# Attention with its scores held transposed, in a four-layer graph network kernel

## The chip, the cores and the metric

The kernel runs on one core of one Trainium2 chip. A core has five engines that work side by side, each through its own queue in order: TensorE (PE in the profile; the loading of its weights is shown apart as PEld), VectorE (DVE), ScalarE (ACT), GpSimd (POOL) and SyncE (SP), which here only starts DMAs. POOL starts DMAs too. SBUF is the on-chip memory with 128 partitions; PSUM is the small memory that TensorE writes its products to[...]. The metric is the device time of one execution in microseconds, lower is better.

## The reference

There are 2708 nodes with 512 features each, and a symmetric 0/1 adjacency matrix with about 0.6% ones. Four layers follow each other; each is `x = layernorm(x + layer(x, adj))`. Layers 0, 1 and 3 multiply the adjacency matrix with x (or with x scaled by the degrees) and then with a 512 x 512 weight matrix. The change is in layer 2, which is two rounds of attention over all pairs of nodes:

```python
def _gat_layer(x, W, adj):              # W: 512 x 1024
    proj = x @ W
    Wh, Ws = jnp.split(proj, 2, axis=-1)
    scores = Wh @ Ws.T                  # 2708 x 2708
    a = jax.nn.softmax(scores, axis=-1) * adj
    out = a @ Wh
    out = out + x
    return jax.nn.leaky_relu(out, 0.01)
x = inputs
for l in range(2):
    x = _gat_layer(x, W_stack[l], adj)
```

The softmax runs over the whole row, before the mask. Its denominator is therefore the sum over all 2708 columns, and not only over the neighbours.

## The kernel before

**Layers 0, 1 and 3** are `aggregated`. It holds x as row blocks of 128 nodes, split into a high and a low part (`xh`, `xl`, both in the fp32r format). The nodes that are summed into are cut into six chunks of at most 512 columns (`CH`: three of 512, two of 384, one of 404). For each chunk the transposed adjacency matrix is loaded by SP in six pieces (`at`, line 476), made into `m` by a copy (line 489), and TensorE adds up four PSUM accumulators `acc` (line 493), with x as the stationary and the adjacency as the moving operand. So the result is transposed, features down the partitions. `project` (line 453) multiplies it with the weights, which turns it back to rows, and the epilogue (`end0`, `end1`, `end3`) does bias, residual and layernorm on DVE. In layers 0 and 1 the rows are written to DRAM (`saved`, line 524), and the next layer loads them again (`xr`, line 383, and `xres`, line 450).

**Layer 2** is `attention`. It loads the 22 row blocks of x, and for each of its two rounds goes through three stages:

- *Projection* (lines 224 to 232). Per row block: four transposes of x (`tr_x`), a copy `xt`, eight matmuls with the halves of W (`mm_ws`, `mm_wh`), the copies `ws` and `z` (the Wh of this block), four transposes of `ws`, and a copy into `wst`, which holds Ws transposed.
- *Scores and softmax* of a row block of 128 queries: `z` is transposed (`wht`, line 143), six column chunks of 452 are multiplied into PSUM (`sp`, line 147), and DVE copies each to the score matrix `s` and takes its row maximum in the same instruction (line 154). Queries lie on the partitions, so the row maximum is one number per partition, `nmax`. ACT takes one exponential over 2708 columns with `nmax` as bias and adds up the row sums on the way (line 172). SP loads the mask and DVE multiplies it in (line 177).
- *Weighing* (`weigh`). The second product needs the keys on the partitions. So the 22 blocks of `s` are transposed on TensorE in groups of four (`etr`, line 191), copied to SBUF by ACT and DVE in turn (`et`), and used as the stationary operand against `z` (`acc`, line 202). `finish` divides by the row sum, adds x and applies the leaky ReLU; in the second round it also adds the layer's input, takes the layernorm and stores the block (lines 210 to 219).

The scores of row block i+1 stand in TensorE's queue before the weighing of block i. All matmuls of this layer are in Float32. A scheduler decides the order in which the instructions stand in each engine's queue, from the dependencies and the order in which they are written. A pool hands out buffers: a tile with `bufs=n` has n buffers in turn, and a new tile waits until the one that used its buffer before is finished with. Between two of the kernel's stages, the pools of the new stage take the memory of the old stage's pools, and wait for all of them.

Of the kernel before, what the change touches and what calls it, by code (L numbers as in the profile page):

```python
# [8 lines left out]
FP = mybir.dt.float32  # L9
# [3 lines left out]
AF = mybir.ActivationFunctionType  # L13
ALU = mybir.AluOpType
AX = mybir.AxisListType
PSUM = bass.MemoryType.PSUM
DRAM = bass.MemoryType.DRAM

P = 128
N = 2708  # L20
D = 512
NB = 22
NP = NB * P
DC = D // P
BANK = 512

CH = [(0, 512), (512, 512), (1024, 512), (1536, 384), (1920, 384), (2304, 404)]
# [7 lines left out]
SLOPE = 0.01  # L35


def rows_of(i):
    return min(P, N - i * P)


class Kernel:


    def __init__(self, ctx, tc, x_in, x_t, adj, adj_t, w0, b0, w1, b1, w2, w3, b3, out):
        self.tc, self.nc = tc, tc.nc
        nc = self.nc
# [17 lines left out]
            [scratch.tile([P, D], FP, tag=f"x{s}_{i}", name=f"x{s}_{i}") for i in range(NB)]  # L65
            for s in range(3)
        ]

# [291 lines left out]
    def aggregated(self, layer, source, weights, bias, epilogue):  # L360
# [4 lines left out]
        with ExitStack() as ctx:  # L365
            pool = lambda name, bufs, **kw: ctx.enter_context(
                tc.tile_pool(name=f"{name}{layer}", bufs=bufs, **kw)
            )
# [3 lines left out]
            ps_mm = pool("ps_mm", 2, space=PSUM)  # L372
            ps_deg = pool("ps_deg", 1, space=PSUM)
            w = self.load_w(hp, weights, D, f"w_{layer}")
            bt = hp.tile([P, D], FP, tag="bias", name=f"bias{layer}")
# [69 lines left out]
            def project(k, ht):  # L445
                c0, cw = CH[k]
                for q in range(-(-cw // P)):
# [4 lines left out]
                    for c in range(DC):  # L452
# [6 lines left out]
                        )  # L459
                    epilogue(i, n, ps, bt, xr)  # L460

            done = None
            for k, (c0, cw) in enumerate(CH):
# [9 lines left out]
                for g, (b0, b1) in enumerate(GROUPS):  # L473
# [26 lines left out]
                    if g == 0 and done is not None:  # L500
                        project(*done)
                ht = hp.tile([P, DC, BANK], FP, tag="ht", name=f"ht{layer}_{k}")
                if layer == 0:
# [6 lines left out]
                done = (k, ht)  # L510
            project(*done)

    def fast(self):
# [20 lines left out]
        def end1(i, n, ps, bt, x):  # L534
            r = self.rows.tile([P, D], FP, tag="r", name=f"r1_{i}")[:n]
            nc.vector.scalar_tensor_tensor(
                r, ps[:n], self.dis[:n, i : i + 1], bt[:n], ALU.mult, ALU.add
            )
            nc.vector.tensor_add(r, r, x[:n])
            normalized(i, n, r, self.saved[1])  # L540

# [8 lines left out]
        self.aggregated(1, self.saved[0], self.w1, self.b1, end1)  # L550
        self.attention(self.saved[1], self.saved[2])
        self.aggregated(3, self.saved[2], self.w3, self.b3, end3)
# [75 lines left out]
```

## Time and profile before

| what | value |
|---|---|
| three runs | 3170.51, 3165.39, 3166.81 us; median 3166.81 |
| profiled run | 3169.31 us, its span 3167.5 us, mean granted TensorE clock 0.984 |
| layers 0 and 1 | 0 to about 660 us of the span |
| attention, first round | TensorE from 671.7 us to 1755 us |
| attention, second round | from 1755 us to 2834 us |
| layer 3 | from 2855 us to the end |
| DMA | 236.93 MB, 75 GB/s over the span |

The profile is one execution. Its page lists the busy time of each engine, the span in 40 slices, the chain of work that ended last (followed back from the last instruction, at each step to what released it), and the costliest groups of instructions. A group's row has its line, engine and operation, output and inputs with their shapes, the count, then the busy time in us, the mean of one in ns, and the idle time of the engine ahead of it. Matmuls overlap in a pipeline and their ends are modelled, so the distance between their starts tells more of their cost than their mean duration.

### The profile page before, as it was taken

How to read it: one execution, taken by the hardware profiler on the slowest of the kernel's cores; microseconds unless marked ns; L12 is line 12 of the kernel's file. 1: busy time of each engine (PE TensorE's matmuls, PEld its weight loads, DVE VectorE, ACT ScalarE, POOL GpSimd, SP SyncE). 2: the span in 40 equal slices, each digit the busy share in tenths (PEclk: the TensorE clock that was granted, in tenths of full speed). 3: DMA queues.
4: the chain of work that ended last, by engine and by line, in shares of the span. 5: the costliest groups of instructions: out<-in, count | busy, mean ns of one | idle time of the engine just before them, and what ended most of it. 6: DMA issues, size and time to landing. Idle time of an engine off the chain costs nothing.

```text
span 3167.5 us, 25252 instructions
## 1 busy us (share of the span) xinstructions
PE 3017.2 (95%) x9974; PEld 1746.5 (55%) x9974; DVE 1057.7 (33%) x2511; ACT 552.9 (17%) x668; POOL 188.9 (6%) x314
## 2 busy tenths in 40 slices
PE   6999799979999999999999999999999999979997
PEld 5677577844454554444444444544444444436785
DVE  7768423221122222222222112333333333333133
ACT  3112332211110011111111111111111111114221
POOL 3112201010000000000000000000000000002000
PEclk9999899989999999999999999999999999999998
DMA  7434654420011111111111000111111111116441
GB/s 256 151 129 143 218 174 131 133 104 0 11 51 35 36 35 35 36 35 36 35 36 35 0 0 18 49 49 49 47 47 45 49 49 49 49 51 239 140 147 58
DMA packets 115138, 236.93 MB, mean 75 GB/s; under 512 B 10406, under 2 KB 69542, under 8 KB 115008
## 3 DMA queue, kind: packets, MB, share of 16 engines
q1 hardware_dynamic: 90432, 152.54, 14.9%
q0 software_dynamic: 24576, 82.68, 7.6%
q8 instruction: 80, 1.31, 0.2%
q14 instruction: 50, 0.41, 0.0%
HBM read 212.32 MB, written 22.85 MB: 74 GB/s over the span
## 4 chain that ended last, share of the span: by engine, by line
PE 89%; DVE 4%; issue 3%; DMA 2%; ACT 1%; POOL 0%; POOLq 0%; SPq 0%; ACTq 0%; DVEq 0%
PE acc L202 26%; PE sp L147 26%; PE acc L493 18%; PE mm L453 6%; PE mm_ws L111 5%; PE mm_wh L111 5%; PE etr L191 2%; DMA xr<-x 1%; DVE r L210 1%; ACT xt L226 1%; DVE wht L143 1%; DMA xr<-in_x 1%; PE tr_x L104 1%; PE tr_ws L104 1%; DVE odd L398 0%
## 5 line engine op out<-in xcount | busy, mean ns | idle before, releaser
L202 PE MATMUL acc<-z,et 128*128 128x512 f32 x1936 | 867.6, 593 | 0.2
L147 PE MATMUL sp<-wst,wht 128*128 128x452 f32 (+1 forms) x2112 | 810.9, 544 | 6.1 <-DVE wht L143 0.8
L493 PE MATMUL acc<-m,xh 128*128 128x512 f32 (+2 forms) x1584 | 592.6, 375 | 69.1 <-DMA xr<-x 21.3
L147 PEld LDWEIGHTS sp<-wst,wht 128*128 128x128 f32 x2112 | 397.8, 190 | 398.8 <-issue 382.4
L493 PE MATMUL acc<-m,xl 128*128 128x512 f32 (+2 forms) x1584 | 584.9, 371 | 6.5 <-DVE xl L386 6.5
L202 PEld LDWEIGHTS acc<-z,et 128*128 128x128 f32 x1936 | 353.8, 190 | 373.7 <-issue 372.6
L493 PEld LDWEIGHTS acc<-m,xh 128*128 128x128 f32 x1584 | 304.2, 192 | 109.0 <-ACT xh L385 43.8
L154 DVE TENSOR_SCALAR_CACHE_REDUCE s<-sp 128x452 f32<-128x452 f32 (+1 forms) x264 | 165.8, 628 | 554.2 <-PE sp L147 554.2
L493 PEld LDWEIGHTS acc<-m,xl 128*128 128x128 f32 x1584 | 303.6, 192 | 46.4 <-DVE xl L386 11.0
L172 ACT ACTIVATE s<-s,nmax 128x2708 f32<-128x2708 f32 x44 | 112.3, 2552 | 723.0 <-DVE nmax L171 723.0
L453 PE MATMUL mm<-w,ht 128*128 128x512 f32 (+1 forms) x528 | 231.6, 596 | 3.2 <-DVE ht L507 3.2
L195 ACT COPY et<-etr 128x512 f32<-128x512 f32 x132 | 77.4, 586 | 750.6 <-PE etr L191 750.6
L193 DVE COPY et<-etr 128x512 f32<-128x512 f32 x132 | 79.2, 600 | 350.7 <-PE etr L191 350.6
L111 PE MATMUL mm_ws<-w,xt 128*128 128x512 f32 x352 | 165.4, 613 | 31.9 <-ACT xt L226 31.9
L191 PEld LDWEIGHTS etr<-ident,s 128*128 128x128 f32 x968 | 118.4, 141 | 94.6 <-issue 94.6
L453 PEld LDWEIGHTS mm<-w,ht 128*128 128x128 f32 (+1 forms) x528 | 98.2, 187 | 125.0 <-issue 112.7
L111 PE MATMUL mm_wh<-w,xt 128*128 128x512 f32 x352 | 158.2, 592 | 0.0
L489 ACT CAST m<-at 128x2048 fp32r<-128x2048 f32 (+2 forms) x72 | 113.4, 1577 | 222.9 <-PE acc L493 206.0
L177 DVE TENSOR_TENSOR s<-s,gat_a 128x452 f32<-128x452 f32 (+1 forms) x264 | 145.3, 619 | 0.0
L191 PE MATMUL etr<-ident,s 128*128 128x128 f32 x968 | 141.6, 273 | 0.0
L111 PEld LDWEIGHTS mm_ws<-w,xt 128*128 128x128 f32 x352 | 64.2, 192 | 107.3 <-issue 64.8
L215 POOL DMA_DIRECT2D xb<-x x22 | 11.9, 539 | 1831.4 <-DVE r L217 1791.3
(90 smaller groups left out, 1392.3 us busy)
## 6 DMA issues: line engine op xcount, KB each, us to landing
gat_a<-in_adj SPq DMA_DIRECT2D x220, 226.0 KB, 3.5
at<-in_adj_t SPq DMA_DIRECT2D x45, 1024.0 KB, 5.1
at<-in_adj_t SPq DMA_DIRECT2D x30, 768.0 KB, 4.4
at<-in_adj_t SPq DMA_DIRECT2D x15, 808.0 KB, 4.5
x<-o POOLq DMA_DIRECT2D x44, 256.0 KB, 2.5
xr<-x POOLq DMA_DIRECT2D x44, 256.0 KB, 5.1
xres<-x POOLq DMA_DIRECT2D x44, 256.0 KB, 2.9
x<-x POOLq DMA_DIRECT2D x44, 256.0 KB, 3.4
```

Of the source, the lines that this page charges most:

```text
L111: self.nc.tensor.matmul(ps, src[:, c, :], w[:, c, lo : lo + D], start=(c == 0), stop=(c == DC - 1))
L147: nc.tensor.matmul(sp[:, :cw], wht[:, c, :], wst[:, c, c0 : c0 + cw], start=(c == 0), stop=(c == DC - 1),)
L154: nc.vector.tensor_scalar(s[:, c0 : c0 + cw], sp[:, :cw], 1.0, None, ALU.mult, ALU.max, accum_out=mx[:, k : k + 1],)
L172: nc.scalar.activation(s[:, :N], s[:, :N], AF.Exp, bias=nmax, accum_out=den)
L177: nc.vector.tensor_mul(s[:, c0 : c0 + cw], s[:, c0 : c0 + cw], a[:, :cw])
L191: nc.tensor.transpose(ps[:, q, :], s[:, bass.ts(c, P)], self.ident)
L193: nc.vector.tensor_copy(et[:, :n, :], ps[:, :n, :])
L195: nc.scalar.copy(et[:, :n, :], ps[:, :n, :])
L202: nc.tensor.matmul(acc, et[:, q, :], z[c], start=(c == 0), stop=(c == NB - 1))
L453: nc.tensor.matmul(ps[:n], ht[:, c, q * P : q * P + n], w[:, c, :], start=(c == 0), stop=(c == DC - 1),)
L489: nc.scalar.copy(m[:, :nb, :cw], at[:, :nb, :cw])
L493: nc.tensor.matmul(acc[d][:, :cw], x[j][:, bass.ts(d, P)], m[:, j - b0, :cw], start=(j == 0 and x is xh), stop=(j == NB - 1 and x is xl),)
```

## The change

Attention is written anew as `scored`, and layer 1 hands x over in another form.

- **Scores transposed.** The work goes by the six chunks `CH` of queries, and within a chunk by 22 blocks j of 128 keys. `sp` has the keys on the partitions and up to 512 queries along the columns. A step's score tile goes to one of 26 buffers of `ring` by an ACT copy; the chunk's 22 tiles are all held, because the maximum over the keys must be known first.
- **Row maxima by transposes.** DVE keeps a running maximum over the tiles (`top`). At the end of a chunk `shift_rows` transposes it on TensorE, reduces it on DVE and spreads it over 128 columns (`wide`); `shift_columns` transposes that back, so that each query's maximum stands on all partitions (`shift`).
- **Softening.** Per tile: DVE subtracts `shift`, ACT takes the exponential, POOL adds it to the running sum `sum`, DVE multiplies by the mask, which SP loads per tile from the transposed adjacency matrix.
- **Second product.** `weigh` uses the masked exponentials as they lie as the moving operand, with slices of `z` as the stationary one, into four accumulators over the key blocks. The transposes `etr` and the copies `et` are gone. `close` sums `sum` over the partitions by a product with ones (`den`), takes the reciprocal, and multiplies, adds x and applies the leaky ReLU on tiles of 128 x 4 x cw, on DVE and POOL.
- **x kept transposed.** In layer 1 the normalized rows stay in SBUF (`lasting`); `turn` transposes them chunk by chunk and stores them to `turned[0]`. The projection loads this form, so that it transposes neither x nor Ws. The first round stores its result to `turned[1]`. In the second round `rows_back` transposes the result to rows for the layernorm and stores them for layer 3.
- **Pools** of `aggregated` and `scored` are opened with `reuse_waits="tile"`: a tile that takes memory of an earlier stage waits only for the tiles that lay there.

The steps are interleaved by hand: at step t the scores of step t, the weighing of step t-25 and the softening of step t-23 are written.

```diff
-                tc.tile_pool(name=f"{name}{layer}", bufs=bufs, **kw)
+                tc.tile_pool(name=f"{name}{layer}", bufs=bufs, reuse_waits="tile", **kw)
...
+            lasting = pool("lasting", 5) if layer == 1 else None
...
+            def turn(k):
+                c0, cw = CH[k]
+                t = ap.tile([P, DC, BANK], FP, tag="xt", name=f"x2t{k}", bufs=1)
+                for q, o in enumerate(finished):
+                    n = min(P, cw - q * P)
+                    ps = ps_deg.tile([P, DC, P], FP, tag="deg", name=f"tr_x2_{k}_{q}")
+                    for c in range(DC):
+                        nc.tensor.transpose(
+                            ps[:, c, :n], o[:n, bass.ts(c, P)], self.ident[:n, :n]
+                        )
+                    nc.scalar.copy(t[:, :, q * P : q * P + n], ps[:, :, :n])
+                nc.gpsimd.dma_start(self.turned[0][k], t[:, :, :cw])
+                finished.clear()
...
+                    if g == 2 and finished:
+                        turn(k - 1)
...
+            keep, ring, work = pool("keep", 1), pool("ring", 26), pool("work", 1)
+            ps_acc = pool("ps_acc", 1, space=PSUM)
+            ps_mm, ps_tr = pool("ps_mm", 2, space=PSUM), pool("ps_tr", 2, space=PSUM)
...
+            def project(layer):
+                w = []
+                for c in range(2 * DC):
+                    t = ring.tile([P, D], FP, tag="s", name=f"w2_{layer}_{c}")
+                    half = bass.ts(c // DC, D)
+                    nc.sync.dma_start(t, self.w2[layer, bass.ts(c % DC, P), half])
+                    w.append(t)
+                for k, (c0, cw) in enumerate(CH):
+                    xt = load_xt(layer, k)
+                    for m in range(DC):
+                        ps = ps_mm.tile([P, BANK], FP, tag="mm", name=f"wst{layer}_{k}_{m}")
+                        for c in range(DC):
+                            nc.tensor.matmul(
+                                ps[:, :cw],
+                                w[DC + c][:, bass.ts(m, P)],
+                                xt[:, c, :cw],
+                                start=(c == 0),
+                                stop=(c == DC - 1),
+                            )
...
+                    for q in range(-(-cw // P)):
+                        i, n = c0 // P + q, min(P, cw - q * P)
+                        ps = ps_mm.tile([P, D], FP, tag="mm", name=f"z{layer}_{i}")
+                        for c in range(DC):
+                            nc.tensor.matmul(
+                                ps[:n],
+                                xt[:, c, q * P : q * P + n],
+                                w[c],
+                                start=(c == 0),
+                                stop=(c == DC - 1),
+                            )
...
+            def turn_wh(layer, k):
+                c0, cw = CH[k]
+                wht = work.tile([P, DC, BANK], FP, tag="wht", name=f"wht{layer}_{k}")
+                for q in range(-(-cw // P)):
+                    i, n = c0 // P + q, min(P, cw - q * P)
+                    ps = ps_tr.tile([P, DC, P], FP, tag="tr", name=f"tr_wh{layer}_{i}")
+                    for c in range(DC):
+                        nc.tensor.transpose(
+                            ps[:, c, :n], z[i][:n, bass.ts(c, P)], self.ident[:n, :n]
+                        )
+                    to = wht[:, :, q * P : q * P + n]
+                    if q % 2:
+                        nc.vector.tensor_copy(to, ps[:, :, :n])
+                    else:
+                        nc.scalar.copy(to, ps[:, :, :n])
+                return wht
...
+            def scores(ch, j):
+                n, cw = rows_of(j), ch.cw
+                ps = ps_mm.tile([P, BANK], FP, tag="mm", name=f"sp{ch.name}_{j}")
+                for c in range(DC):
+                    nc.tensor.matmul(
+                        ps[:n, :cw],
+                        wst[j][:, c, :n],
+                        ch.wht[:, c, :cw],
+                        start=(c == 0),
+                        stop=(c == DC - 1),
+                    )
+                s = ring.tile([P, BANK], FP, tag="s", name=f"s{ch.name}_{j}")
+                ch.s.append(s)
+                nc.scalar.copy(s[:n, :cw], ps[:n, :cw])
+                if j == 1:
+                    ch.top = work.tile([P, BANK], FP, tag="top", name=f"top{ch.name}", bufs=2)
+                    nc.vector.tensor_max(ch.top[:, :cw], ch.s[0][:, :cw], s[:, :cw])
+                elif j > 1:
+                    nc.vector.tensor_max(ch.top[:n, :cw], ch.top[:n, :cw], s[:n, :cw])
+            def shift_rows(ch):
+                nq = -(-ch.cw // P)
+                ps = ps_tr.tile([P, DC, P], FP, tag="tr", name=f"tr_top{ch.name}")
+                for q in range(nq):
+                    n = min(P, ch.cw - q * P)
+                    nc.tensor.transpose(
+                        ps[:n, q, :], ch.top[:, q * P : q * P + n], self.ident
+                    )
+                mx = self.small.tile([P, DC], FP, tag="mx", name=f"mx{ch.name}")
+                wide = work.tile([P, DC, P], FP, tag="wide", name=f"wide{ch.name}")
+                for q0, q1, n in ((0, ch.cw // P, P), (ch.cw // P, nq, ch.cw % P)):
+                    if q0 == q1:
+                        continue
+                    nc.vector.tensor_reduce(mx[:n, q0:q1], ps[:n, q0:q1, :], AX.X, ALU.max)
+                    nc.vector.tensor_copy(
+                        wide[:n, q0:q1, :],
+                        mx[:n, q0:q1].unsqueeze(2).to_broadcast([n, q1 - q0, P]),
+                    )
+                ch.wide = wide
+            def shift_columns(ch):
+                ps = ps_tr.tile([P, BANK], FP, tag="tr", name=f"tr_mx{ch.name}")
+                for q in range(-(-ch.cw // P)):
+                    n = min(P, ch.cw - q * P)
+                    nc.tensor.transpose(
+                        ps[:, q * P : q * P + n], ch.wide[:n, q, :], self.ident[:n, :n]
+                    )
+                ch.shift = work.tile([P, BANK], FP, tag="shift", name=f"shift{ch.name}", bufs=2)
+                nc.scalar.copy(ch.shift[:, : ch.cw], ps[:, : ch.cw])
+            def soften(ch, j):
+                n, cw = rows_of(j), ch.cw
+                s = ch.s[j][:n, :cw]
+                c0 = CH[ch.k][0]
+                a = work.tile([P, BANK], FP, tag="a", name=f"a{ch.name}_{j}", bufs=4)
+                nc.sync.dma_start(a[:n, :cw], self.adj_t[j * P : j * P + n, c0 : c0 + cw])
+                nc.vector.tensor_sub(s, s, ch.shift[:n, :cw])
+                nc.scalar.activation(s, s, AF.Exp)
+                if j == 0:
+                    ch.sum = work.tile([P, BANK], FP, tag="sum", name=f"sum{ch.name}", bufs=2)
+                    nc.gpsimd.tensor_copy(ch.sum[:, :cw], s)
+                else:
+                    nc.gpsimd.tensor_add(ch.sum[:n, :cw], ch.sum[:n, :cw], s)
+                nc.vector.tensor_mul(s, s, a[:n, :cw])
+            def weigh(ch, j):
+                n, cw = rows_of(j), ch.cw
+                if j == 0:
+                    ch.acc = [
+                        ps_acc.tile([P, BANK], FP, tag=f"acc{d}", name=f"acc{ch.name}_{d}")
+                        for d in range(DC)
+                    ]
+                for d in range(DC):
+                    nc.tensor.matmul(
+                        ch.acc[d][:, :cw],
+                        z[j][:n, bass.ts(d, P)],
+                        ch.s[j][:n, :cw],
+                        start=(j == 0),
+                        stop=(j == NB - 1),
+                    )
+            def close(ch):
+                layer, k, cw = ch.layer, ch.k, ch.cw
+                o = work.tile([P, DC, BANK], FP, tag="o", name=f"o{ch.name}")
+                for d in range(DC):
+                    nc.scalar.copy(o[:, d, :cw], ch.acc[d][:, :cw])
+                xt = load_xt(layer, k)
+                ps = ps_tr.tile([P, BANK], FP, tag="tr", name=f"den{ch.name}")
+                nc.tensor.matmul(
+                    ps[:, :cw], self.ones, ch.sum[:, :cw], start=True, stop=True
+                )
+                r = work.tile([P, BANK], FP, tag="r", name=f"r{ch.name}")
+                nc.vector.reciprocal(r[:, :cw], ps[:, :cw])
+                o = o[:, :, :cw]
+                nc.vector.tensor_mul(o, o, r[:, :cw].unsqueeze(1).to_broadcast([P, DC, cw]))
+                nc.gpsimd.tensor_add(o, o, xt[:, :, :cw])
+                nc.vector.scalar_tensor_tensor(o, o, SLOPE, o, ALU.mult, ALU.max)
+                if layer == 0:
+                    nc.gpsimd.dma_start(self.turned[1][k], o)
+                    return
+                first = load_xt(0, k)
+                nc.gpsimd.tensor_add(o, o, first[:, :, :cw])
+                ch.o = o
+            def rows_back(ch):
+                c0, cw = CH[ch.k]
+                for q in range(-(-cw // P)):
+                    i, n = c0 // P + q, min(P, cw - q * P)
+                    ps = ps_tr.tile([P, D], FP, tag="tr", name=f"tr_o{i}")
+                    for c in range(DC):
+                        nc.tensor.transpose(
+                            ps[:n, bass.ts(c, P)], ch.o[:, c, q * P : q * P + n], self.ident
+                        )
+                    t = work.tile([P, D], FP, tag="row", name=f"row{i}", bufs=2)
+                    if n < P:
+                        nc.gpsimd.memset(t, 0.0)
+                    self.layernorm(t[:n], ps[:n])
+                    nc.gpsimd.dma_start(self.saved[2][i], t)
+            LAG = 3
+            for layer in range(2):
+                project(layer)
+                chunks = [Chunk(layer, k) for k in range(len(CH))]
+                chunks[0].wht = turn_wh(layer, 0)
+                steps = [(ch, j) for ch in chunks for j in range(NB)]
+                for t in range(len(steps) + NB + LAG + 1):
+                    if t < len(steps):
+                        ch, j = steps[t]
+                        scores(ch, j)
+                        if j == NB - 1 and ch.k + 1 < len(chunks):
+                            chunks[ch.k + 1].wht = turn_wh(layer, ch.k + 1)
+                    if t >= NB and t % NB == 0 and t // NB <= len(chunks):
+                        shift_rows(chunks[t // NB - 1])
+                    u = t - NB - LAG
+                    if 0 <= u < len(steps):
+                        weigh(*steps[u])
+                    if t >= NB and t % NB == 0 and t // NB <= len(chunks):
+                        shift_columns(chunks[t // NB - 1])
+                    v = t - NB - 1
+                    if 0 <= v < len(steps):
+                        soften(*steps[v])
+                    if 0 <= u < len(steps) and steps[u][1] == NB - 1:
+                        close(steps[u][0])
+                    if layer == 1 and u >= NB and u % NB == 2:
+                        rows_back(chunks[u // NB - 1])
+                if layer == 1:
+                    rows_back(chunks[-1])
...
-            normalized(i, n, r, self.saved[1])
+            o = self.lasting.tile([P, D], FP, tag="x2", name=f"x2_{i}")
+            self.layernorm(o[:n], r)
+            return o
...
-        self.attention(self.saved[1], self.saved[2])
+        self.scored()
```

## The prediction

> **What bounds the kernel now.** I read the page first: busy time, then slices, then the chain, then the groups.
>
> ```profile
> PE 3017.2 (95%) x9974; PEld 1746.5 (55%) x9974; DVE 1057.7 (33%) x2511; ACT 552.9 (17%) x668; POOL 188.9 (6%) x314
> ...
> PEclk9999899989999999999999999999999999999998
> ...
> PE 89%; DVE 4%; issue 3%; DMA 2%; ACT 1%; POOL 0%; POOLq 0%; SPq 0%; ACTq 0%; DVEq 0%
> PE acc L202 26%; PE sp L147 26%; PE acc L493 18%; PE mm L453 6%; PE mm_ws L111 5%; PE mm_wh L111 5%; PE etr L191 2%; DMA xr<-x 1%; DVE r L210 1%; ACT xt L226 1%; DVE wht L143 1%; DMA xr<-in_x 1%; PE tr_x L104 1%; PE tr_ws L104 1%; DVE odd L398 0%
> ...
> L202 PE MATMUL acc<-z,et 128*128 128x512 f32 x1936 | 867.6, 593 | 0.2
> L147 PE MATMUL sp<-wst,wht 128*128 128x452 f32 (+1 forms) x2112 | 810.9, 544 | 6.1 <-DVE wht L143 0.8
> ...
> L191 PE MATMUL etr<-ident,s 128*128 128x128 f32 x968 | 141.6, 273 | 0.0
> ```
>
> TensorE is on 89% of the chain; in both attention layers it is simply full. The others have room, so only TensorE's own work, and new waits on it, count. The means of 593 and 544 ns are overlapped records, so I price by starts, from the chain of one row block:
>
> ```profile
> 968.25 18.44 PE sp L147 x48
> 986.69 3.43 PE acc L202 x8
> 990.12 0.44 PE etr L191 x4
> ...
> 1007.15 0.75 DVE r L210
> 1007.90 0.61 DVE wht L143
> 1008.51 0.04 issue
> 1008.55 3.68 PE sp L147 x9
> ```
>
> The period is 1008.55-968.25 = 40.30 us: 48 score instructions in 18.44 (0.384 each), 44 weighing ones at 3.44/8 = 0.430 (18.92), and 2.94 for 26 transposes, 0.113 each with their small waits. In the projection a row block takes (859.45-684.75)/20 = 8.735 us, by the mm_ws starts of the chain. A Float32 matmul is two instructions.
>
> The stage's end, from the timeline:
>
> ```profile
> 2833.51 0.75 DVE L210 SCALAR_TENSOR_TENSOR r<-acc,rden,x 128x512 f32<-128x512 f32 x1 [4.66 <-PE acc L202]
> ...
> 2841.55 38.27 SPq L476 DMA_DIRECT2D at<-in_adj_t  x7
> ...
> 2843.38 2.13 POOL L383 DMA_DIRECT2D xr<-x  x4
> ...
> 2854.75 0.80 PE L493 MATMUL acc<-m,xh 128*128 128x512 f32 x1 [21.28 <-DMA xr<-x]
> ```
>
> TensorE stands 21.3 us here; the last store gates the next stage's loads.
>
> POOL's price comes from the groups by form:
>
> ```profile
> L429 POOL TENSOR_TENSOR xt<-xt,dg 128x512 f32<-128x512 f32 x12 | 17.3, 1471 | 65.4 <-DVE cnt_sb L440 65.4
> ```
>
> **What the Trainium skill says.** *Perfetto Trace Analysis*, "Tensor Engine Instruction (MATMUL, LD_WEIGHTS)": a matmul's end is an estimate. The trace agrees: a transpose is shown as 273 ns and starts every 110. *FP8 and Floating Point Precision*, "TensorE Precision Notes": true Float32 takes four passes; the trace has two instructions of 430 ns for 512 columns. *SBUF — State Buffer*, "SBUF: two separate sides": a VectorE operation with two SBUF inputs and a GpSimd operation that reads SBUF exclude each other for their whole length. No row of before shows it; it bounds the slow end below. *VectorE: DVE Perf Modes*, "First, the fixed hardware budget": the reciprocal iterates with a repeat count of 8 at 0.96 GHz; an estimate for 512 columns is 4.3 us. The trace has it only on 1 to 4 columns (0.16 us).
>
> **The change, part by part**, on TensorE, both layers together.
>
> *Scores.* Four products per key block over 2708 queries, as many columns and instructions as before: 0.
>
> *Transposes of the exponentials.* 968 go: -968 x 0.113 = -109.4. Their 264 copies on ACT and DVE lay beside TensorE: 0.
>
> *Second product.* 22 x 4 x 2708 columns instead of 22 x 22 x 512, as 2112 instructions instead of 1936. At the score price, 2112 x 0.384 = 811.4 against 44 x 18.92 = 832.5: -21.1. Narrow 384-column chunks are not in the trace for Float32; if the overhead stays 4 ns instead of 8, 8 us less on each product.
>
> *Projection.* Before 44 x 8.735 = 384.3. Now per layer 192 instructions at 0.384 and 176 at 0.430 = 149.5, no transposes; both 299.0: -85.3. Its eviction (0.59 ACT, 0.69 DVE, or four quarter pieces) stays under the 3.4 us of a product and is hidden.
>
> *Added on TensorE.* Row maxima there and back, 88 transposes: +9.9. Column sums, 24 instructions: +9.2. Output turned back, 88: +9.9. x turned in layer 1, 88, of which 72 lie in its dense part: +8.1. Together +37.1. The sum so far: -178.7.
>
> *Softening.* A step (one key block, 512 queries) gives TensorE 16 x 0.430 = 6.9 us, DVE three operations of 0.69 (2.1), ACT a copy of 0.59 and an exponential of some 0.5, POOL an addition of 1.47, SP one 256 KB load (3.5 us to land). Even one after the other DVE and POOL take 3.5. In the built order softening also runs several steps ahead of weighing. I take 0; below it is impossible, since TensorE is full; above, see the slow rival.
>
> *Turning x (layer 1).* One PSUM buffer: each group of transposes waits for ACT's copy (0.59) of the one before, with 4 to 6 matmuls of 0.22 between. About 1 us per chunk: +5 (0 to 12).
>
> *Chunk seams.* wht has one buffer and acc one set: at a chunk's start the scores wait for four copies, at its end the next weighing for one copy of acc. Mostly three to seven products lie between. 1.5 us at each layer's start, 1 at its first seam, 0.5 at the others, rounded up to 8 a layer: +16 (5 to 40).
>
> *Rows back (second layer).* In the built queue TensorE reaches the turned-back output three steps after a chunk's last weighing. By then must have passed: ACT's four copies 2.3, reciprocal 0.7 to 4.3, DVE product 2.3 (a 2048-column operation, L398, took 2.29), POOL's addition 4 x 1.47 = 5.9, DVE 2.3, POOL again 5.9: 19.4 to 23 us, plus what is queued ahead. Three steps are 20.6 us for the first chunk, 18.2 and 15.7 for the next, 15.9 against a chain three quarters as long, and four weigh-only steps of 2.75 for the fifth. The waits are 0-5, 2-7, 4-9, 0-3, 4-8: I take 16. The second pair of blocks waits for a pair's layernorm in two PSUM buffers, 2 to 3 us: 10. Behind TensorE everything else is queued, so it counts: +26 (5 to 50).
>
> *Start of attention.* x comes turned, chunk by chunk. But in SP's queue the weight loads w2 stand behind a mask load whose buffer waits for the last layernorm, and the fourth of them for the last turned store. On before's clock: layernorm 663.7, transposes and copy 664.8, store landing some 4 us later, five loads to about 674.5. TensorE began at 671.7: +3 (-5 to +6).
>
> *Between the layers.* xt and w2 are there early; DVE's and POOL's closing (some 12 us) lies beside 27 us of projection: 0.
>
> *Layer 0 to 1.* Buffers are waited for one by one, but the first at load waits for DVE's last ht, where it started before (336.5); xr now stands behind the last store in POOL's queue, 5 us later, with less traffic beside it: 0 (-5 to +5).
>
> *End of attention.* After the last weighing (404 columns): copies 0.8, reciprocal about 2, DVE 1.8, POOL 4.0, DVE 1.8, POOL 4.0, transposes 0.9, two paired layernorms about 10, then POOL's w, bias and xr issues (1.9) and their landing, 5; xh and xl 1.3: about 35 us against 21.3, +14. The at loads and casts are then already in, which saves about 4 of the uneven start: +10 (0 to +18).
>
> Waits together +60. Net -178.7+60 = -119: 3167.5-119 = 3049 on the profile's span. The profiled run took 3169.3, the others 3165.4 to 3170.5 (median 3166.8), so span and median agree within 1 us.
>
> **Rivals.** *Waits vanish* (the order leaves more slack than I count; reciprocal 0.7): 18 us of waits remain instead of 60, 3007. For it: every wait stands behind work that I estimated. Against: TensorE takes its queue in order. *Long closings:* reciprocal at 4.3 and POOL and DVE excluding each other stretch both layers' seams and the end by 4 us at each of 11 closings: 3094. *Slower than before:* the exclusion makes the softening step the bound. Where both products run (220 steps, TensorE 6.15 us on average), DVE's 1.9 plus POOL's addition must exceed 6.15; the gain is gone when they reach 6.7, so POOL's addition must take 4.8 us instead of 1.3 (1.47 at 452 of 512 columns). At 5.0 the step is 6.9: 3049+220 x 0.75 = 3214. Against: POOL's row, taken in layer 0, is 1.47 with DVE 75% busy. *The turned x saves nothing*, its weights being late: already in my sum, but should the seams cost the whole gain, no change.
>
> **How the numbers follow.** My sum 0.45 (alone 3025 to 3075), waits vanish 0.23, long closings 0.26, no change 0.02, slower 0.04. So faster 0.94, same 0.02, slower 0.04, where 0.2% is about what a measurement can tell from no change. The range 2998 to 3105 takes in both neighbours.
>
> **What would show it.** Right: no etr; acc and sp 2112 instructions each at starts 0.38 apart on average; layers of about 992 and 1025 us against 1084 and 1078; short TensorE waits on tr_o and 35 us ahead of layer 3; DVE and POOL well under 60% busy. Wrong: TensorE waiting in every step for DVE's masked product, or POOL additions over 3 us.

## The result, and the profile after

The changed kernel takes 3194.22 us (median of four runs, 3192.33 to 3195.24) against 3168.38 us before: a ratio of 1.0082, with a 95% interval of 1.0064 to 1.0099. The forecast was 3049, with a range of 2998 to 3105 and a chance of 0.04 for slower. So the range does not hold the time, and the sign is wrong.

The page of the kernel after, first the busy times, the granted clock, and the groups that answer to those shown of before:

```profile
PE 2921.0 (91%) x9150; PEld 1688.7 (53%) x9150; DVE 1345.0 (42%) x2229; ACT 639.7 (20%) x1080; POOL 615.4 (19%) x568
...
PEclk9999899989999999999999999998989898988999
...
L636 PE MATMUL sp<-wht,wst 128*128 128x512 f32 (+4 forms) x2112 | 866.7, 558 | 46.2 <-ACT s L645 46.2
L709 PE MATMUL acc<-s,z 128*128 128x512 f32 (+4 forms) x2112 | 853.9, 549 | 14.9 <-ACT o L721 9.3
...
L698 POOL TENSOR_TENSOR sum<-sum,s 128x512 f32<-128x512 f32 (+4 forms) x252 | 351.3, 1394 | 124.6 <-ACT s L693 110.0
...
L699 DVE TENSOR_TENSOR s<-s,a 128x512 f32<-128x512 f32 (+3 forms) x264 | 304.4, 1188 | 21.1 <-POOL sum L698 16.7
L692 DVE TENSOR_TENSOR s<-s,shift 128x512 f32<-128x512 f32 (+3 forms) x264 | 240.4, 960 | 35.8 <-ACT shift L683 35.8
```

TensorE has less work (2921 us against 3017), `etr` is gone, and the two products have their 2112 instructions each. But TensorE is no longer full: its share fell from 95% to 91%, and the granted clock drops again and again in attention, where it stayed at 9 before once the first round was under way. The two DVE rows are the odd ones, and their means mix widths. Kept apart by width, an operation on two SBUF tiles took in the kernel before:

```profile
L177 DVE TENSOR_TENSOR s<-s,gat_a 128x452 f32<-128x452 f32 x220 | 121.7, 619 | 0.0
L545 DVE TENSOR_TENSOR r<-r,xres 128x512 f32<-128x512 f32 x21 | 14.5, 690 | 0.2
```

In the kernel after, at 512 columns:

```profile
L698 POOL TENSOR_TENSOR sum<-sum,s 128x512 f32<-128x512 f32 x120 | 189.6, 1580 | 68.4 <-ACT s L693 61.4
L699 DVE TENSOR_TENSOR s<-s,a 128x512 f32<-128x512 f32 x126 | 158.8, 1295 | 9.2 <-POOL sum L698 8.1 <-DMA a<-in_adj_t 1.1
L692 DVE TENSOR_TENSOR s<-s,shift 128x512 f32<-128x512 f32 x126 | 124.0, 1034 | 20.4 <-ACT shift L683 20.4
```

The mask product takes 1.30 us and the subtraction 1.03, where 0.69 was to be expected. POOL's additions, at 1.58, are near the 1.47 that they were priced at.

The same by stage: start and end, length, then busy time (and instructions) of PE, PEld, DVE, ACT, POOL, and the clock. First the two rounds of attention and the stretch ahead of layer 3, in the kernel after:

```profile
684.00:1727.20 1043.20, 999.74 (x2625) 487.43 (x2626) 413.67 (x483) 178.74 (x363) 211.87 (x153) 0.98 0.14 45
1727.20:2855.00 1127.80, 1016.35 (x2696) 502.70 (x2695) 467.36 (x648) 197.11 (x394) 250.66 (x179) 0.94 0.15 46
2855.00:2890.30 35.30, 4.73 (x19) 2.99 (x19) 15.17 (x40) 8.71 (x11) 13.29 (x13) 0.53 0.54 183
```

By TensorE's starts, attention began 12 us later than before (684.0 against 671.7). The first round took 1043 us instead of 1084, where 992 were forecast. The second took 1163 with the stretch ahead of layer 3, where before needed 1099.5 and the forecast was 1060; layer 3 was 9.6 us shorter (303.1 against 312.7). The sum, +12.3 - 40.4 + 63.6 - 9.6, is the 26 us between the spans. TensorE stands idle for 1043.2 - 999.7 = 43.5 us in the first round and 111.4 us in the second, at a clock of 0.98 and 0.94.

Whom it waits for, from TensorE's waits (sum in us, times, longest):

```profile
PE tr_o L747 <- POOL o L737: 54.7, 6, 13.9
PE sp L636 <- ACT s L645: 46.2, 12, 7.8
...
PE tr_o L747 <- DVE row L106: 36.5, 5, 14.6
...
PE tr_o L747 <- DVE ln_r L95: 17.4, 1, 17.4
```

The `tr_o` waits are 108.7 us in all; 17.2 of them belong to the last chunk, after which there is nothing else to do. A closing shows where they come from. This is the timeline of all engines around the first one of the second round, with only the lines of the closing and of what stands beside it:

```profile
2147.41 3.35 DVE L728 RECIPROCAL r<-den 128x512 f32<-128x512 f32 x1
...
2153.58 4.89 POOL L731 TENSOR_TENSOR o<-o,xt 128x2048 f32<-128x2048 f32 x1 [4.62 <-DVE o L730]
2154.03 4.99 DVE L699 TENSOR_TENSOR s<-s,a 128x512 f32<-128x512 f32 x1
...
2159.65 1.23 ACT L693 ACTIVATE s<-s 128x512 f32<-128x512 f32 x2 [11.62 <-DVE s L692]
...
2162.51 4.87 POOL L737 TENSOR_TENSOR o<-o,xt 128x2048 f32<-128x2048 f32 x1 [3.19 <-DVE o L732]
2162.94 4.98 DVE L650 TENSOR_TENSOR top<-top,s 128x512 f32<-128x512 f32 x1
...
2167.43 1.97 PE L747 MATMUL tr_o<-ident,o 128*128 128x128 f32 x8 [7.84 <-POOL o L737]
```

Here POOL twice adds 2048 columns, and beside each addition a VectorE operation of 512 columns takes 5 us instead of 0.68: it ends 0.55 us, about its own length, after POOL does. All nine of POOL's 2048-column additions have such a partner (4.85 to 5.00 us), and it starts 0.26 to 0.45 us after POOL. The product `s<-s,a` has no data in common with `o<-o,xt`. Behind it on VectorE stand the subtractions, behind them ACT's exponentials (11.62 us of idle time), and behind these in ACT's queue the copies of the next scores. From `den` (2135.0) to the last addition (2167.4) the closing takes 32 us; the forecast had 19 to 23.

### The profile page after: what moved, and what is told of

The parts are those of the page before. It is cut to its first block, busy times and chain, and to the rows that moved or that the text cites. A ratio compares the mean times of both kernels' runs of the same rounds, so it can differ in the third digit from the quotient of the medians.

```text
span 3193.4 us, 24534 instructions
## 1 busy us (share of the span) xinstructions
PE 2921.0 (91%) x9150; PEld 1688.7 (53%) x9150; DVE 1345.0 (42%) x2229; ACT 639.7 (20%) x1080; POOL 615.4 (19%) x568
## 5 line engine op out<-in xcount | busy, mean ns | idle before, releaser
L636 PE MATMUL sp<-wht,wst 128*128 128x512 f32 (+4 forms) x2112 | 866.7, 558 | 46.2 <-ACT s L645 46.2
L709 PE MATMUL acc<-s,z 128*128 128x512 f32 (+4 forms) x2112 | 853.9, 549 | 14.9 <-ACT o L721 9.3
L636 PEld LDWEIGHTS sp<-wht,wst 128*128 128x128 f32 (+1 forms) x2112 | 402.1, 192 | 474.6 <-issue 302.7
L709 PEld LDWEIGHTS acc<-s,z 128*128 128x128 f32 (+1 forms) x2112 | 401.3, 192 | 408.7 <-issue 238.0
L650 DVE TENSOR_TENSOR top<-top,s 128x512 f32<-128x512 f32 (+2 forms) x240 | 168.2, 701 | 828.0 <-ACT s L645 827.1
L698 POOL TENSOR_TENSOR sum<-sum,s 128x512 f32<-128x512 f32 (+4 forms) x252 | 351.3, 1394 | 124.6 <-ACT s L693 110.0
L520 PEld LDWEIGHTS acc<-m,xh 128*128 128x128 f32 x1584 | 303.0, 191 | 101.1 <-ACT xh L394 46.4
L699 DVE TENSOR_TENSOR s<-s,a 128x512 f32<-128x512 f32 (+3 forms) x264 | 304.4, 1188 | 21.1 <-POOL sum L698 16.7
L692 DVE TENSOR_TENSOR s<-s,shift 128x512 f32<-128x512 f32 (+3 forms) x264 | 240.4, 960 | 35.8 <-ACT shift L683 35.8
L578 PE MATMUL wst<-xt,w 128*128 128x512 f32 (+2 forms) x384 | 151.9, 555 | 12.3 <-DMA w<-in_w 12.3
L596 PE MATMUL z<-w,xt 128*128 128x512 f32 (+1 forms) x352 | 153.2, 592 | 0.0
L747 PE MATMUL tr_o<-ident,o 128*128 128x128 f32 (+1 forms) x88 | 22.2, 426 | 108.7 <-POOL o L737 54.7
```

Of the source, the lines that this page charges most:

```text
L520: nc.tensor.matmul(acc[d][:, :cw], x[j][:, bass.ts(d, P)], m[:, j - b0, :cw], start=(j == 0 and x is xh), stop=(j == NB - 1 and x is xl),)
L578: nc.tensor.matmul(ps[:, :cw], w[DC + c][:, bass.ts(m, P)], xt[:, c, :cw], start=(c == 0), stop=(c == DC - 1),)
L596: nc.tensor.matmul(ps[:n], xt[:, c, q * P : q * P + n], w[c], start=(c == 0), stop=(c == DC - 1),)
L636: nc.tensor.matmul(ps[:n, :cw], wst[j][:, c, :n], ch.wht[:, c, :cw], start=(c == 0), stop=(c == DC - 1),)
L650: nc.vector.tensor_max(ch.top[:n, :cw], ch.top[:n, :cw], s[:n, :cw])
L692: nc.vector.tensor_sub(s, s, ch.shift[:n, :cw])
```

## The experiments

Three theories were put against each other. **A:** only the place of `rows_back` in the order is wrong, three steps being too few. **B:** VectorE and GpSimd exclude each other, and that holds up the chain from softening to closing. **C:** VectorE is simply short of time. All times are medians; the kernel before stood at 3167 to 3168 us beside each.

**Rows back later** (`e1_late`).

```diff
-                    if layer == 1 and u >= NB and u % NB == 2:
+                    if layer == 1 and u >= NB and u % NB == 12:
```

> Only the place of rows_back in the order: ten steps later (u % NB == 12 instead of 2). Theory A (queue place: TensorE reaches tr_o before the closing chain is done): the tr_o waits of the first five chunks go, 108.7 - 17.2 (the last chunk, which stays) = 91.5 us, and with them some 10 us of TensorE at half clock: 3194 - 100 = about 3094. Theory B (VectorE and GpSimd exclude each other, and the softening is behind because of it): the stalls were also time in which VectorE caught up, so half of it comes back as waits of sp for the copies s: about 3145. Both agree on the first half of attention (no change).

Measured: 3143.11 us, ratio to before 0.9917 (0.9900 to 0.9933). The first round is as it was (684.4 to 1728.5). The first five chunks' waits on `tr_o` are gone, but TensorE's waits now read:

```profile
PE sp L636 <- ACT s L645: 81.7, 19, 14.1
```

That is 81.7 us where it was 46.2: of the 91.5 us of `tr_o` waits, 35.5 came back as waits for the score copies. The kernel gained 51 us, B's half (3145) and not A's whole (3094): the place decides where TensorE stands, and the chain behind it is late wherever it stands.

**The sum on VectorE, the closing's additions on VectorE, and both** (`e2_sumdve`, `e3_closedve`, `e4_nopool`).

```diff
-                    nc.gpsimd.tensor_copy(ch.sum[:, :cw], s)
+                    nc.vector.tensor_copy(ch.sum[:, :cw], s)
...
-                    nc.gpsimd.tensor_add(ch.sum[:n, :cw], ch.sum[:n, :cw], s)
+                    nc.vector.tensor_add(ch.sum[:n, :cw], ch.sum[:n, :cw], s)
```

```diff
-                nc.gpsimd.tensor_add(o, o, xt[:, :, :cw])
+                nc.vector.tensor_add(o, o, xt[:, :, :cw])
...
-                nc.gpsimd.tensor_add(o, o, first[:, :, :cw])
+                nc.vector.tensor_add(o, o, first[:, :, :cw])
```

The first pair of edits alone:

> Only the running sum moved from GpSimd to VectorE (264 additions of about 0.69 us more on VectorE, 182 us). Theory B (exclusion): the subtractions and mask products fall from 0.96 and 1.19 us to about 0.65; TensorE's waits of sp for s (46 us) fall below 15, the tr_o waits by some 10 us a chunk, half clock by half: about 3194 - 31 - 50 - 20 = 3093. Theory A (queue place alone): the chain of the closing is as long as before, about 3190. Theory C (VectorE is the engine that is short): slower, about 3194 + 30.

The second pair alone:

> Only the additions of the closing (2048 columns, 4.9 us each on GpSimd, 18 of them) moved to VectorE at about 2.3 us. Theory B: each closing is shorter by 2.6 us per addition and VectorE is no longer held for 5 us by each: tr_o waits -8 us on each of 6 chunks, sp waits from 46 to about 25: about 3120. Theory A: only 2 x 2.6 us on each of 6 chunks: about 3162. Theory C: slower, about 3200.

Both:

> Both: the running sum and the closing's additions on VectorE, GpSimd only starts DMAs in attention. Theory B: no VectorE operation above its length alone; sp waits under 10 us, tr_o waits of the first five chunks under 20 us together, mean clock 0.975: about 3194 - 40 - 75 - 25 = 3055. Theory A: as with the closing's additions alone, about 3162. Theory C: slower than with either alone.

| kernel | us | ratio to before (95%) |
|---|---|---|
| sum on VectorE | 3043.02 | 0.9598 (0.9582 to 0.9614) |
| closing's additions on VectorE | 3128.63 | 0.9873 (0.9856 to 0.9889) |
| both | 2990.48 | 0.9432 (0.9417 to 0.9448) |

More work for VectorE makes the kernel faster by 204 us, so C is out, and A's 3190 and 3162 are too. B has the direction each time; it was close for the closing (3120 expected), and its gain was 50 us too small for the sum and 65 too small for both. The two edits give 151 and 66 us alone and 204 together: two costs that nearly add. VectorE's mask product is back at its length alone:

```profile
L699 DVE TENSOR_TENSOR s<-s,a 128x512 f32<-128x512 f32 x126 | 86.6, 688 | 0.3
```

The stages of the kernel with both, with the same columns as above:

```profile
683.30:1667.30 984.00, 982.82 (x2625) 484.68 (x2626) 363.66 (x620) 182.15 (x363) 10.34 (x16) 0.99 0.16 48
1667.30:2654.90 987.60, 986.00 (x2697) 488.95 (x2695) 413.69 (x791) 208.55 (x401) 21.77 (x36) 0.99 0.17 53
```

TensorE runs the same instructions, and is idle for 1.2 and 1.6 us. Against the kernel after, the first round is 59.2 us shorter, of which 42.3 was idle time and 16.9 slower matmuls; the second, up to its last weighing, is 140.2 us shorter, 109.8 idle and 30.4 slower matmuls.

**Unrelated work on GpSimd** (`e5_shadow`, `e6_shadowcopy`). Moving the sum took away two things: what GpSimd does beside VectorE, and a wait, since the mask product overwrites the tile that GpSimd reads. Here the first is put back without the second, on top of the kernel with both edits; its second form has `tensor_copy(b, a)` instead.

```diff
                 nc.vector.tensor_mul(s, s, a[:n, :cw])
+                b = work.tile([P, BANK], FP, tag="b", name=f"b{ch.name}_{j}")
+                nc.gpsimd.tensor_add(b[:n, :cw], a[:n, :cw], a[:n, :cw])
```

> The kernel with all additions on VectorE, and 264 extra GpSimd additions of the same shape that read only the mask tile and write a tile that nobody reads; the result is not touched. It parts two reasons why the sum on GpSimd cost so much. Theory B1 (GpSimd's and VectorE's additions exclude each other): VectorE's subtractions and products rise from 0.62 us to 0.9 or more although nothing depends on GpSimd, and the time rises from 2990 towards the 3129 of the run with only the closing's additions moved: 3070 to 3130. Theory B2 (the mask product overwrites the tile that GpSimd still reads, so it waits in the queue for it): lengths stay at 0.62, time 2985 to 3000.

> As the run before, but the extra GpSimd operation is a copy of the mask tile (one input) instead of an addition. Theory B1 as stated for any GpSimd operation that reads SBUF: VectorE's two-input operations are stretched too, by the shorter length of a copy (0.96 us against 1.58): 3020 to 3070. If only GpSimd operations with two inputs take part: 2985 to 3000.

Measured: 3042.22 us (3034.59 to 3052.08) with the additions and 3006.18 (3001.06 to 3007.52) with the copies, against 2990.48. From the groups by form of the run with additions:

```profile
L699 DVE TENSOR_TENSOR s<-s,a 128x512 f32<-128x512 f32 x126 | 101.6, 807 | 17.4 <-DMA a<-in_adj_t 17.1
...
L701 POOL TENSOR_TENSOR b<-a 128x512 f32<-128x512 f32 x126 | 254.9, 2023 | 635.0 <-DMA a<-in_adj_t 628.9 <-POOL b L701 0.2
```

Without the extra work the product takes 0.69 us at this width, and the GpSimd addition takes 1.47 in layer 0 of the same run. Now both are longer, though neither reads what the other writes. Copies that read one tile do it too, by less (the product at 0.75). Both times fall outside what was expected: B1's bands began at 3070 and 3020, the other answer ended at 3000. So GpSimd's work lengthens VectorE's on unrelated data too, and a wait through the tile is not needed for it. With the additions the whole costs 52 us, and these may include that GpSimd holds the mask tiles longer: VectorE waits 26.7 us for mask loads, where it waited 2.2 without the additions. The run with only the closing's additions moved stands at 3129, so 86 us of the sum's cost were still open.

**The wait alone, and the sum without the wait** (`e9_tie`, `e10_apart`). The first keeps all additions on VectorE and lets the product wait for GpSimd; the second leaves the sum on GpSimd and takes the wait away.

```diff
+                b = work.tile([P, 2 * BANK], FP, tag="b", name=f"b{ch.name}_{j}")
+                e = work.tile([P, 2], FP, tag="e", name=f"e{ch.name}_{j}", bufs=2)
+                nc.gpsimd.tensor_copy(e[:n, 0:1], s[:, 0:1])
+                nc.gpsimd.memset(b, 0.0)
+                nc.gpsimd.tensor_copy(e[:n, 1:2], s[:, 1:2])
                 nc.vector.tensor_mul(s, s, a[:n, :cw])
```

```diff
-            keep, ring, work = pool("keep", 1), pool("ring", 26), pool("work", 1)
+            keep, ring, work = pool("keep", 1), pool("ring", 25), pool("work", 1)
...
-                a = work.tile([P, BANK], FP, tag="a", name=f"a{ch.name}_{j}", bufs=4)
+                a = work.tile([P, BANK], FP, tag="a", name=f"a{ch.name}_{j}", bufs=7)
...
-                nc.vector.tensor_mul(s, s, a[:n, :cw])
+                nc.vector.tensor_mul(a[:n, :cw], s, a[:n, :cw])
+                ch.s[j] = a
```

> The kernel with all additions on VectorE; per tile GpSimd reads one column of the exponentials, clears a scratch tile of 1024 columns (about 1 us, it reads nothing), and reads another column. The mask product, which overwrites the exponentials, has to wait for GpSimd as it did with the sum there, but GpSimd hardly reads SBUF. If that wait in VectorE's queue is what the extra GpSimd additions on unrelated data left unexplained (3129 with the sum on GpSimd, 3042 with unrelated additions), then 3040 to 3080 with VectorE's lengths near 0.62. If only the exclusion counts: 2985 to 3005.

> The sum stays on GpSimd and the closing's additions are on VectorE (3129 before this edit), but the mask product is written to the mask's tile and weighed from there, so that it need not wait for GpSimd's reading (the mask tiles become 7, the ring 25). If the wait through the tile is the rest: about 3042, as with unrelated additions. If the exclusion in step with the chain is: 3100 to 3130.

Measured: 2993.98 us (2992.18 to 2995.24) and 3098.59 (3097.47 to 3099.20). The first lies where the exclusion alone was expected, the second 1.4 us below the band of the exclusion in step. In the first, GpSimd is busy for about 2 us per tile and the product has to wait for it; by the groups by form it keeps its length:

```profile
L704 DVE TENSOR_TENSOR s<-s,a 128x512 f32<-128x512 f32 x126 | 86.4, 686 | 4.1 <-POOL e L703 3.4
```

In the second, it waits for no sum, and still:

```profile
L699 DVE TENSOR_TENSOR a<-s,a 128x512 f32<-128x512 f32 x126 | 128.3, 1029 | 282.3 <-DMA a<-in_adj_t 272.9 <-PE sp L636 9.4
L692 DVE TENSOR_TENSOR s<-s,shift 128x512 f32<-128x512 f32 x126 | 126.1, 1053 | 20.6 <-ACT shift L683 20.6
```

So 2 us of GpSimd per tile that hardly read SBUF cost 3.5 us in all. But VectorE waited only 4.4 us for GpSimd in that run, where it waited 43 us for the sum in the run with only the closing's additions moved; what a wait of that size costs is not shown. In the second, the sum on GpSimd costs 108 us (3098.6 against 2990.5), twice what the unrelated additions cost, but not all of it need be the exclusion: a mask tile now comes free only after its weighing, so VectorE waits 481 us for mask loads, and the same edit with the sum on VectorE was not run. Nor is it shown where the other 30 us of 3128.6 went. VectorE's rows fit a higher price in step with the chain: there the subtraction and the product take 1.05 and 1.03, while beside the unrelated additions, which follow the mask loads, 0.77 and 0.81.

**The start and the end of attention** (`e7_w2`, `e8_best`), on top of the kernel with both edits. The first loads `w2` from ScalarE's queue, the half that is read first ahead; the second also takes `xr` from SyncE's queue.

```diff
-                w = []
-                for c in range(2 * DC):
-                    t = ring.tile([P, D], FP, tag="s", name=f"w2_{layer}_{c}")
+                w = [None] * (2 * DC)
+                for c in (4, 5, 6, 0, 7, 1, 2, 3):
+                    w[c] = ring.tile([P, D], FP, tag="s", name=f"w2_{layer}_{c}")
+                for c in (4, 5, 6, 7, 1, 2, 3, 0):
                     half = bass.ts(c // DC, D)
-                    nc.sync.dma_start(t, self.w2[layer, bass.ts(c % DC, P), half])
-                    w.append(t)
+                    nc.scalar.dma_start(w[c], self.w2[layer, bass.ts(c % DC, P), half])
...
-                nc.gpsimd.dma_start(xr, source[j])
+                (nc.sync if layer else nc.gpsimd).dma_start(xr, source[j])
```

> The kernel with all additions on VectorE, and the attention weights w2 issued from ScalarE's queue instead of behind the mask loads in SyncE's, the half that the first product reads first. If the 12 us that TensorE waits for w at the start of attention come from that queue and order, the wait falls to 2 to 6 us: 2980 to 2985. If they come from the DMA engines' bandwidth or from the turned x, it stays: 2988 to 2992.

> As the run before, and in layers 1 and 3 the loads xr of the rows come from SyncE's queue, not behind the last stores in GpSimd's. If the 13.5 us that TensorE waits for xh ahead of layer 3 come from that queue place, most of them go (the first row blocks were stored 200 us earlier): 2965 to 2975. If they come from the closing chain, which stays: 2978 to 2985.

Measured: 2988.14 us (2985.25 to 2989.11), no difference that can be told from 2990.48, though the wait for `w` fell from 12.0 to 6.7 us; and 2982.09 (2980.49 to 2982.99), ratio to before 0.9415 (0.9402 to 0.9428). Both lie where the other answer expected them. Yet in the second, TensorE's wait for `xh` ahead of layer 3 falls from 13.7 us (the run before it) to 1.9, so the queue place was the reason for that wait; layer 1, whose rows come from SyncE's queue too, starts at 354.9 instead of 364.8. But layer 3 then needs 311.9 us instead of the 303.0 of the kernel with both edits. Of these 8.9 us, 3.9 lie ahead of the last store's issue: TensorE waits 2.0 us for `xl`, behind conversions `xh` that wait for single `xr` loads, which follow one another in SyncE's queue. The other 4.9 lie behind it, where GpSimd's last DRAIN takes 5.46 us instead of 1.13; why, the runs do not show. This is the best version of the case: 5.9% faster than before, 6.6% faster than the change as it was made.

## Why the prediction was wrong, by its steps

- **TensorE's work: right.** Without the turning of x, which lies in layer 1, the forecast for the two rounds without waits was -178.7 - 8.1 = -186.8 us; with GpSimd out of the way they are 190.2 shorter than before. That the span as a whole is 2989.4 where 3167.5 - 178.7 = 2988.8 were forecast is luck: attention starts 11.6 us later than before, 10.2 more pass ahead of layer 3, and layer 3 is 9.7 shorter. The projection took 151 us in the first round and 150 in the second by its starts (149.5 forecast). A matmul starts every 0.430 us at 512 columns and every 0.322 at 384 (2.574 for eight), so the average was 0.379, not 0.384.
- **Softening: the step that failed.** The prediction took 0 ("Even one after the other DVE and POOL take 3.5" us of the 6.9 us of a step). As a rate this holds: VectorE is busy for 414 of 1043 us in the first round. But the queues are in order and the chunks come in bursts: when a chunk's maximum is known (`shift`, at 1081.5 us for the second chunk), VectorE has many tiles to subtract and multiply, its timeline shows no idle time until 1143, and many of its operations stand for as long as a GpSimd addition runs. ACT's exponentials wait for them, the copies of the next scores wait behind the exponentials, and TensorE waits for those copies. Latency at the seams decided, not the rate. Neither sign that the prediction had named for being wrong appeared: TensorE waited once for a masked product, 5.4 us, and the additions to the sum took 1.39 us on the mean, one of them over 3. Whether softening written further ahead of the weighing would have hidden it was not tried. The timeline of the kernel after shows such a burst in its first round:

```profile
1123.01 14.67 POOL L698 TENSOR_TENSOR sum<-sum,s 128x512 f32<-128x512 f32 x9
...
1124.77 10.12 DVE L692 TENSOR_TENSOR s<-s,shift 128x512 f32<-128x512 f32 x6
...
1135.46 0.57 ACT L645 COPY s<-sp 128x512 f32<-128x512 f32 x1
```

  Six subtractions take 10.12 us, 1.69 each, beside additions of 1.63 (14.67 / 9). The last exponential and the copy of the scores follow, and TensorE, which needs that copy, starts at 1136.08 after 7.81 us of waiting. In place of 0, moving the sum away is worth 138 us (3128.6 to 2990.5): at least part of it is VectorE held by GpSimd's reading, and how much the wait for the sum adds is open.
- **The slow rival had the right cause and the wrong price.** It cited the Trainium skill (*SBUF — State Buffer*, "SBUF: two separate sides") for the exclusion, and then asked how long POOL's addition must become, 4.8 us. POOL's additions took 1.58; VectorE was the one that stood, as the page allows: whoever starts first has the ports for its whole instruction. The trace agrees in the closing, where VectorE starts second and takes 4.99 us instead of 0.68. In the burst it agrees less plainly: one addition and one subtraction together take 1.67 us, less than the 1.47 + 0.69 of the two alone. As "against" the prediction named POOL's 1.47 in layer 0 with VectorE 75% busy, which said nothing about VectorE's side.
- **Rows back and seams: far too small.** +26 and +16 stood for the waits; measured were 91.5 us on `tr_o` in the first five chunks, 46.2 on `s`, 14.9 on `acc`. The reciprocal, at 3.35 us, lay within its bounds. The closing's additions held VectorE for up to 5 us each, which the 19 to 23 us of the chain did not count; moving these 18 instructions is worth 53 us (3043.0 to 2990.5). With GpSimd out of the way, the `tr_o` waits outside the last chunk are 0.4 us.
- **The clock: not in the sum.** After most of the long waits the matmuls run slower for a while (shown at the end): for the same instructions TensorE is busy for 47 us longer in both rounds together (16.9 + 30.4) than in the kernel with GpSimd out of the way.
- **Up to the start of attention: 12.3 us where 16.1 were counted, but in other parts.** From layer 0 to layer 1 it is 5.7 us (365.2 instead of 359.6), where 0 (-5 to +5) was forecast. Layer 1, from its start to its last layernorm, is 1.5 us longer, where the turning of x stood in the sum with 8.1 of work and 5 of waits. From that layernorm to TensorE's first instruction of attention 13.0 us pass instead of 8.0, 5.1 more where 3 (-5 to +6) was forecast: the eight `w2` loads were issued from 672.1 to 682.1, with a wait of 5.8 us for the last turned store among them, and the half needed first came last. Earlier and reordered, TensorE's wait for `w` halves, with little to show in the total.
- **End of attention: right, then luck.** 35.3 us from the last weighing to layer 3 were measured where 35 were forecast. Layer 3 gained 9.6 us afterwards, not 4, but only 1.3 of them come before the last store is issued (296.5 us against 297.8). Behind it 6.7 us pass instead of 15.0, which no term of the prediction covers; why, the runs do not show.

## What to carry to other kernels

Before work is put on GpSimd because it is idle, look at what VectorE does at that moment: in this kernel VectorE's operations on two SBUF tiles stood while GpSimd read SBUF, up to 5 us beside a GpSimd addition of 4.9. The waiting showed as a longer VectorE row and hardly as idle time, so compare a row's length at one width with its length elsewhere. A share of 42% busy says nothing about latency; price a chain through in-order queues by its longest path in a burst. Here TensorE also lost more than the waits themselves, 47 us of slower matmuls beside 152 us of idle time. When a moved step gives back only half of its wait, the chain behind it may be late, and that is where to look.

## What the runs showed of the hardware that was not expected

- Many waits of TensorE are followed by slow matmuls, and not only waits go with them. The timeline of TensorE in the kernel after:

```profile
1136.08 5.70 PE L636 MATMUL sp<-wht,wst 128*128 128x512 f32 x8 [7.81 <-ACT s L645]
1141.62 3.60 PE L709 MATMUL acc<-s,z 128*128 128x512 f32 x8
```

  After 7.81 us of waiting, eight matmuls take 5.70 us instead of 3.60. The Trainium skill (*TensorE: Matmul & The Clock Gate*, "HAM oscillation — how this bites in real kernels") describes waits that throttle the array again; the clock of 0.94 in the second round, against 0.99 without the waits, agrees. It is no fixed rule of the wait's length: in the first round a wait of 2.5 us was followed by a stretch at half clock, while waits of 3.2 and 3.7 us were not. And with GpSimd out of the way the clock was 0.50 from 1232.4 to 1239.2, though TensorE was busy throughout.
- The exclusion also showed with a GpSimd copy that reads one tile: VectorE's product at 0.75 us and the copy at 1.50 instead of the 0.96 of `sum<-s` in the kernel after (16 us in all). Clearing a tile and reading two single columns, about 2 us of GpSimd per tile, left VectorE's lengths at 0.69.
